# Passes over the ones in the dense part that take their limits from a step on what their block has formed

## The chip, the cores and the metric

The kernel runs on one NeuronCore of a Trainium2 chip. Its engines are PE (TensorE, matrix products and transposes), DVE (VectorE), ACT (ScalarE), POOL (GpSimd) and SP, which issues transfers. The metric is the device time of one launch in microseconds, less is better. Before the change the median of three runs is 2996.88 us (2996.64 to 3000.27).

## What is computed

Four graph layers over 4096 nodes with 256 features share one adjacency matrix of 4096 x 4096 integers. Layer 0 is an attention layer with a dense tail (two normalised hidden layers, a softmax over 128 states and a gate); layer 1 is a mean over neighbours, so it needs the number of ones of each row; layers 2 and 3 are attention layers.

```python
# layer 0, after attention gave h_attn
h_enh = silu(_ln(Wh @ fe1_w + fe1_b, ...)) @ fe2_w + fe2_b
B, C, dt = split(Wh @ W_bcdt + b_bcdt, 3)
ab = softmax(dt + A) * B @ abp_w + abp_b
h_part, z = split((Wh * ab) @ W_hz + b_hz, 2)
hs = ((h_part * silu(z) + h_part * D) @ out_w + out_b) * (1 + C @ cp_w + cp_b)
g = sigmoid(silu(_ln(concat(h_attn, hs) @ g1_w + g1_b, ...)) @ g2_w + g2_b)
out = _ln(g * h_attn + (1 - g) * hs + h_enh, ...)
# layer 1
a = (adj == 1); deg = sum(a, axis=1)
out = (a @ x / deg) @ W.T + b
```

## The kernel before

The rows lie in 32 tiles of 128; four tiles are a block, so there are NB = 8 blocks. Layer 0 first does its attention (to about 624 us), then the dense part, block by block (`dense`, from line 720), then layer 1 follows from about 1220 us.

**The dense part.** `dense(b)` is a generator of some 30 steps. In order it turns the projected rows (`whT`, lines 683 and 687), forms `bc` (line 744) and the exponent of the softmax (line 753), forms `t1` for the hidden layer (line 770) and its normalisation (`fe_off`, `fe_rs`), turns `bc` into `abT` (line 781 then forms `hsT`), turns the normalised `t1` into `zT` with SiLU on ACT (line 710), forms `sz` in two halves (ACT in line 794, POOL in line 797, DVE in line 803), `henh` (line 812) and `hs` (line 819), `comb` (line 684 on ACT, line 687 on DVE), `t2` (line 840) and its normalisation (`gl_off`), again `zT` for the gate, the gate's product and `tanh` (lines 852 to 858), the last normalisation (`ol_off`, line 699 on ACT) and two additions on POOL (lines 861 and 862). `run_staggered(..., 16)` starts a new block every 16 steps, so that the second half of block b-1 stands beside the first half of block b. In the text a pair is such a pair of halves.

**The passes over the ones.** The number of ones of a row is found beside all this. A quarter is 128 rows by 1024 columns of the adjacency matrix. POOL issues its transfer (line 173), and ACT makes two passes over it (line 180): each takes the sign of (value + limit) with the limits -0.5 and -1.5, and adds it up into `over`. Half the difference of the two sums is the count. The first COUNTED = 22 tiles, 88 quarters or 176 passes, are done in the dense part, the others in layer 1. Four buffers hold quarters (AHEAD = 4), one buffer the signs. `with_counts` calls one quarter at each of the first 11 steps of a block (lines 883 to 888).

**What sets the order.** The program is written as above, but the compiler's scheduler fixes the order in each engine's queue, by the dependencies and its own estimate of when each input is there. A pass depends on nothing but its transfer, the buffers and the constant `limits`, so it may be placed ahead of other steps of its block. Each engine then works its queue in that order and waits where an input is late. PSUM buffers matter for PE: three for transposes (`tp`), five for products (`mm`).

Of the kernel before, what the change touches and what calls it, by code (L numbers as in the profile page):

```python
# [11 lines left out]
F32 = mybir.dt.float32  # L12
# [4 lines left out]
ALU = mybir.AluOpType  # L17
# [4 lines left out]
P = 128  # L22
# [6 lines left out]
def run_staggered(gens, period):  # L29

    gens, active, tick = list(gens), [], 0
    while gens or active:
        if gens and tick % period == 0:
            active.append(gens.pop(0))
        for g in list(active):
            if next(g, StopIteration) is StopIteration:
                active.remove(g)
        tick += 1
# [3 lines left out]
def kernel(ctx: ExitStack, tc: tile.TileContext, w: dict, out: bass.AP):  # L42
    nc = tc.nc
# [3 lines left out]
    KD = D // P  # L47
    BT = 4
    NB = NT // BT
# [38 lines left out]
    limits = const.tile([P, 2], F32, name="limits")  # L88
# [63 lines left out]
    def products(ps, lhsT_of, rhs_of, n):  # L152
        for k in range(n):
            nc.tensor.matmul(  # L154
                out=ps, lhsT=lhsT_of(k), rhs=rhs_of(k), start=(k == 0), stop=(k == n - 1)
            )
# [4 lines left out]
    class Tally:  # L161
# [10 lines left out]
                )  # L172
                nc.gpsimd.dma_start(out=self.came[-1], in_=adj[ts(t, P), ts(q, QW)])  # L173

        def count(self, g):
            self.ask(g + self.bufs - 1)
            t, q = self.asked[g]
            for v in range(2):
                sign = self.pool.tile([P, QW], BF16, tag="sign", name="sign", bufs=1)
                nc.scalar.activation(  # L180
                    sign, self.came[g], AF.Sign, bias=limits[:, v : v + 1],
                    accum_out=over[:, t, v, q : q + 1],
                )
# [240 lines left out]
    with ExitStack() as l0:  # L424
# [10 lines left out]
        with ExitStack() as es:  # L435
# [157 lines left out]
            with ExitStack() as ps_:  # L593
                wp = ps_.enter_context(tc.tile_pool(name="l0_w0", bufs=1))
                work = ps_.enter_context(tc.tile_pool(name="l0_prep", bufs=2))
                small = ps_.enter_context(tc.tile_pool(name="l0_ps", bufs=4))
# [51 lines left out]
        with ExitStack() as es:  # L648
            d = es.enter_context(tc.tile_pool(name="l0_d", bufs=1))
            code_p = es.enter_context(tc.tile_pool(name="l0_code", bufs=AHEAD))  # L650
            small = es.enter_context(tc.tile_pool(name="l0_s", bufs=4))
# [27 lines left out]
            def turn(dst, parts, take):  # L679

                ps = pst.tile([P, BW], F32, tag="tp", name="tp")
                for i, part in enumerate(parts):
                    nc.tensor.transpose(ps[:, ts(i, P)], part, ident)
                take(dst, ps)
# [19 lines left out]
            def hidden(z, g, b):  # L704

                zT = d.tile([P, KI, BW], F32, tag="zT", name="zT", bufs=2)
                for k in range(KI):
                    turn(
                        zT[:, k, :], [z[:, i, ts(k, P)] for i in range(BT)],
                        lambda dst, ps: nc.scalar.activation(  # L710
                            dst, ps, AF.Silu, scale=g[:, k : k + 1], bias=b[:, k : k + 1]
                        ),
                    )
                    if k % 2:
                        yield
                return zT

            tally = Tally(code_p, AHEAD, 0, COUNTED)

            def dense(b):  # L720
                at = ts(b, BT)
# [6 lines left out]
                whT = d.tile([P, KD, BW], F32, tag="whT", name="whT", bufs=2)  # L728
                for k in range(KD):
                    turn(  # L730
                        whT[:, k, :], [wh[:, b * BT + i, ts(k, P)] for i in range(BT)],
                        onto,
                    )
                yield
                if b == NB - 1:
                    v0.close()
# [29 lines left out]
                t1 = d.tile([P, BT, DI], F32, tag="t", name="t", bufs=2)  # L766
                for i in range(BT):
                    ps = psm.tile([P, DI], F32, tag="mm", name="mm")
                    products(ps, lambda k: whT[:, k, ts(i, P)], lambda k: fe1[:, k, :], KD)
                    nc.vector.tensor_tensor(t1[:, i, :], ps, fe1_b, ALU.add)  # L770
                    if i % 2:
                        yield
                yield from normed(t1, "fe")
                abT = parts[1, BW][:, 0, :]
                turn(abT, [dt[:, i, :] for i in range(BT)], onto)
                yield
                hsT = parts[KD, BW]
                for k in range(KD):
                    ps = psm.tile([P, BW], F32, tag="mm", name="mm")
                    products(ps, lambda _: abp[:, 0, ts(k, P)], lambda _: abT, 1)  # L780
                    nc.vector.scalar_tensor_tensor(
                        hsT[:, k, :], ps, abp_b[:, k : k + 1], whT[:, k, :], ALU.add, ALU.mult
                    )
                yield
                a1T = yield from hidden(t1, fe_g, fe_b)

                sz = d.tile([P, KI, BW], F32, tag="sz", name="sz")
# [12 lines left out]
                for k in range(KI):  # L800
                    ps = psm.tile([P, BW], F32, tag="mm", name="mm")
                    products(ps, lambda e: whz[:, e, ts(k, P)], lambda e: hsT[:, e, :], KD)
                    nc.vector.scalar_tensor_tensor(
                        sz[:, k, :], ps, hz_b[:, k : k + 1], sz[:, k, :], ALU.add, ALU.mult
                    )
                    if k % 2:
                        yield
                henh = d.tile([P, BT, D], F32, tag="henh", name="henh")
                for i in range(BT):
                    ps = psm.tile([P, D], F32, tag="mm", name="mm")  # L810
                    products(ps, lambda k: a1T[:, k, ts(i, P)], lambda k: fe2[:, k, :], KI)
                    nc.vector.tensor_tensor(henh[:, i, :], ps, fe2_b, ALU.add)
                    if i % 2:
                        yield
                hs = d.tile([P, BT, D], F32, tag="hs", name="hs")
# [65 lines left out]
                    pass  # L881

            def with_counts(b):
                n = COUNTED * NQ // NB
                for k, _ in enumerate(dense(b)):
                    if k < n:
                        tally.count(b * n + k)
                    yield

            tally.ask(AHEAD - 2)  # L890
            run_staggered([with_counts(b) for b in range(NB)], 16)

# [52 lines left out]
    with ExitStack() as es:  # L947
# [10 lines left out]
        small = es.enter_context(tc.tile_pool(name="l1_s", bufs=4))  # L958
# [21 lines left out]
        tally = Tally(over_a, AHEAD, COUNTED, NT)  # L980
# [131 lines left out]
    with ExitStack() as l3:  # L1112
# [4 lines left out]
        with ExitStack() as es:  # L1117
            wp = es.enter_context(tc.tile_pool(name="l3_w", bufs=1))
            work = es.enter_context(tc.tile_pool(name="l3_prep", bufs=2))
            small = es.enter_context(tc.tile_pool(name="l3_ps", bufs=4))  # L1120
# [54 lines left out]
        small = l3.enter_context(tc.tile_pool(name="l3_small", bufs=4))  # L1175
# [165 lines left out]
```

## Time and profile before

| | |
|---|---|
| median of 3 runs | 2996.88 us |
| the profiled execution | 2998.89 us, of which the span 2997.0 us |
| PE busy over the span | 2864.1 us (96%) |
| DVE, ACT, POOL busy | 1878.5, 1282.4, 954.4 us (63, 43, 32%) |
| passes (line 180), all 256 | 293.8 us on ACT, 218 us of them in the dense part |
| dense part, first to last block | about 625 to 1220 us |

The page's second part cuts the span into 40 slices of 75 us, and gives each engine's busy share in tenths. The dense part fills slices 9 to 16:

```profile
PE   6989999999999999899999999999999999999999
DVE  5877666425555554477688788646766566566653
ACT  5765656459997223793163444333212112111211
```

ACT is nearly full in slices 10 to 12 and mostly idle in 14 to 16, while PE is busy in all of them. A busy PE is not a PE at its peak: the ends of matmuls are modelled, and a wait inside a group of matmuls can be counted as busy. So stages are compared by how long the same matmuls take in them. Where the passes fall is seen in windows of one pair each, for the passes of line 180 alone (columns: window and length, ACT busy and instructions, the clock granted to PE, the share of the DMA engines, GB/s; each pass is two instructions):

```profile
630.00:704.00 74.00, 56.68 (x91) 0.98 0.62 92
704.00:778.00 74.00, 50.57 (x83) 1.00 0.52 79
778.00:852.00 74.00, 50.05 (x81) 0.98 0.52 79
852.00:926.00 74.00, 48.77 (x81) 0.98 0.52 79
926.00:1000.00 74.00, 12.18 (x20) 0.98 0.08 18
1000.00:1070.00 70.00, 0.00 (x0) 1.00 0.02 8
1070.00:1140.00 70.00, 0.00 (x0) 1.00 0.03 8
```

### The profile page before, as it was taken

What the parts mean: (1) busy time and instruction counts of PE and PEld (TensorE: products, weight loads), DVE (VectorE), ACT (ScalarE), POOL (GpSimd) and SP (SyncE); (2) the same over time, 40 slices, a digit from 0 to 9 for tenths busy, and PEclk for the clock granted to TensorE, in tenths of its full rate; (3) what the DMA queues carried; (4) which work ended last, traced back from release to release, by engine and by line L of the source; (5) the groups of instructions that cost most, each with busy time, mean ns of one, the idle gap of its engine ahead of it and who ended that gap; (6) DMA issues with size and microseconds to landing.
All of it is one profiled execution on the core that took longest, in us unless ns stands there. A gap on an engine that the chain in (4) does not pass through costs nothing.

```text
span 2997.0 us, 35132 instructions
## 1 busy us (share of the span) xinstructions
PE 2864.1 (96%) x13357; PEld 2334.0 (78%) x13357; DVE 1878.5 (63%) x3456; ACT 1282.4 (43%) x1961; POOL 954.4 (32%) x718
## 2 busy tenths in 40 slices
PE   6989999999999999899999999999999999999999
PEld 5778888866555666687877788888888888888888
DVE  5877666425555554477688788646766566566653
ACT  5765656459997223793163444333212112111211
POOL 4666665534554333220044655550000000000000
PEclk9999999999999999999999999999999999999999
DMA  6966665245553000496332222101111111111100
GB/s 145 213 147 128 132 133 136 67 64 77 78 78 53 8 8 8 122 241 174 123 148 85 78 78 78 43 12 61 64 44 54 38 34 62 39 34 62 34 8 8
DMA packets 109473, 239.41 MB, mean 80 GB/s; under 512 B 10780, under 2 KB 31256, under 8 KB 100600
## 3 DMA queue, kind: packets, MB, share of 16 engines
q1 hardware_dynamic: 68936, 165.44, 15.9%
q0 software_dynamic: 37696, 69.11, 15.4%
q10 hardware_dynamic: 2672, 2.62, 0.3%
q8 instruction: 105, 1.72, 0.2%
q14 instruction: 64, 0.52, 0.1%
HBM read 266.42 MB, written 37.81 MB: 102 GB/s over the span
## 4 chain that ended last, share of the span: by engine, by line
PE 63%; ACT 9%; issue 8%; POOL 7%; DVE 7%; DMA 5%; POOLq 0%; ACTq 0%; DVEq 0%; SPq 0%
PE acc L368 16%; PE acc L1273 15%; PE s L154 15%; PE mm L154 9%; PE acc L1006 5%; POOL y L330 4%; ACT sign L180 4%; DVE run L275 3%; DVE y L326 2%; DMA a<-in_adj_dram 1%; DMA ab_row<-l_ab_d 1%; ACT y L357 1%; DMA turned<-codesT 1%; ACT turned L493 1%; PE q_ps L154 1%
## 5 line engine op out<-in xcount | busy, mean ns | idle before, releaser
L368 PE MATMUL acc<-v,y 128*128 128x257 f32 x4096 | 932.8, 386 | 24.5 <-ACT hp L917 16.0
L368 PEld LDWEIGHTS acc<-v,y 128*128 128x128 f32 x4096 | 774.6, 192 | 139.6 <-ACT hp L917 21.3
L330 POOL TENSOR_TENSOR y<-y,turned 128x1024 f32<-128x1024 f32 (+1 forms) x272 | 550.0, 2036 | 315.5 <-DVE y L326 269.4
L357 ACT ACTIVATE y<-y,sdst 128x512 f32<-128x512 f32 (+1 forms) x544 | 350.8, 689 | 357.3 <-POOL y L330 357.2
L326 DVE SCALAR_TENSOR_TENSOR y<-ab_row,cdst,b 128x512 f32<-128x512 f32 (+1 forms) x544 | 366.4, 710 | 168.8 <-PE acc L368 105.4
L1273 PE MATMUL acc<-v,y 128*128 128x257 f32 x2048 | 454.5, 380 | 0.4 <-DVE rden L1281 0.4
L154 PE MATMUL s<-qT,hT 128*128 128x256 f32 x2048 | 445.2, 379 | 0.7 <-ACT qT L1221 0.7
L1266 ACT ACTIVATE y<-y 128x1024 f32<-128x1024 f32 x128 | 132.2, 1055 | 714.3 <-DVE y L1265 710.1
L154 PEld LDWEIGHTS s<-qT,hT 128*128 128x128 f32 x2048 | 389.2, 190 | 54.0 <-ACT qT L1221 1.4
L1273 PEld LDWEIGHTS acc<-v,y 128*128 128x128 f32 x2048 | 387.3, 190 | 55.7 <-issue 0.8
L180 ACT ACTIVATE sign<-a,limits 128x1024 bf16<-128x1024 bf16 x256 | 293.8, 1148 | 27.2 <-DMA a<-in_adj_dram 21.6
L1235 DVE SCALAR_TENSOR_TENSOR y<-code,s 128x512 f32<-128x512 bf16 x256 | 175.8, 687 | 100.9 <-PE s L154 100.7
L275 DVE SCALAR_TENSOR_TENSOR run<-turned,dst,run 128x512 f32<-128x512 bf16 x248 | 186.7, 753 | 42.1 <-DMA turned<-codesT 37.4
L275 DVE SCALAR_TENSOR_TENSOR run<-turned,v,run 128x512 f32<-128x512 bf16 (+1 forms) x279 | 192.9, 691 | 24.2 <-ACT turned L493 18.5
L1265 DVE TENSOR_TENSOR y<-y,top 128x1024 f32<-128x1024 f32 x128 | 146.2, 1214 | 43.0 <-PE top L1259 43.0
L1242 DVE TENSOR_TENSOR mx<-mx,y 128x512 f32<-128x512 f32 x224 | 154.9, 691 | 7.4
L493 ACT ACTIVATE turned<-cT,log_wide 128x1024 bf16<-128x1024 bf16 x128 | 140.9, 1101 | 30.9 <-PE cT L488 30.6
L1006 PE MATMUL acc<-early,eq 128*128 128x512 f32 x512 | 129.1, 401 | 10.7 <-issue 9.1
L154 PE MATMUL mm<-kept 128*128 128x512 f32 x288 | 136.7, 612 | 1.6 <-DVE kept L687 0.8
L173 POOL DMA_DIRECT2D a<-in_adj_dram x128 | 76.1, 596 | 190.8 <-ACT sign L180 158.2
L1006 PEld LDWEIGHTS acc<-early,eq 128*128 128x128 f32 x512 | 96.8, 190 | 34.3 <-issue 11.2
L1006 PE MATMUL acc<-late,eq 128*128 128x512 f32 x512 | 122.5, 391 | 0.0
(233 smaller groups left out, 2988.9 us busy)
## 6 DMA issues: line engine op xcount, KB each, us to landing
turned<-codesT SPq DMA_DIRECT2D x36, 1024.0 KB
adj_t<-in_adj_dram POOLq DMA_DIRECT2D x128, 256.0 KB, 4.6
codesT<-turned SPq DMA_DIRECT2D x32, 1024.0 KB
a<-in_adj_dram POOLq DMA_DIRECT2D x128, 256.0 KB, 4.7
code<-codesT SPq DMA_DIRECT2D x128, 256.0 KB
code<-codesT SPq DMA_DIRECT2D x64, 512.0 KB
ab_row<-l_ab_d SPq DMA_DIRECT2D x15, 512.0 KB
xt<-in_x_dram SPq DMA_DIRECT2D x8, 512.0 KB
```

The source lines that it names most:

```text
L154: nc.tensor.matmul(out=ps, lhsT=lhsT_of(k), rhs=rhs_of(k), start=(k == 0), stop=(k == n - 1))
L180: nc.scalar.activation(sign, self.came[g], AF.Sign, bias=limits[:, v : v + 1], accum_out=over[:, t, v, q : q + 1],)
L275: nc.vector.scalar_tensor_tensor(st["run"], code, dst, st["run"], ALU.subtract, ALU.min)
L326: nc.vector.scalar_tensor_tensor(y[:, :, k, :], st["ab"][:, 0, :, :], self.cdst[:, c + k : c + k + 1], st["b"], ALU.add, ALU.max,)
L330: nc.gpsimd.tensor_tensor(y, y, mask[:, :, c % QT : c % QT + 2, :], ALU.subtract)
L357: nc.scalar.activation(y[:, :, k, :], y[:, :, k, :], AF.Exp, bias=self.sdst[:, c + k : c + k + 1],)
L368: nc.tensor.matmul(out=acc, lhsT=y[:, r, k, :], rhs=self.v[:, c + k, 0 : D + 1], start=(c + k == 0), stop=(c + k == NT - 1),)
L493: nc.scalar.activation(ct.rearrange("p c i -> p (c i)"), ps, AF.Exp, scale=math.log(UNIT / WIDE), bias=log_wide,)
L1006: nc.tensor.matmul(out=acc, lhsT=eqs[c // (NT // 2)][:, ts(c % (NT // 2), P)], rhs=v1[c // BT][:, c % BT, :, :], start=(c == 0), stop=(c = ...
L1235: nc.vector.scalar_tensor_tensor(y[:, :, c : c + 2, :], st["code"][:, :, c : c + 2, :], -BIG / UNIT, ps, ALU.mult, ALU.add,)
L1242: nc.vector.tensor_tensor(mx, mx, y[:, :, c : c + 2, :], ALU.max)
L1273: nc.tensor.matmul(out=accs[r], lhsT=st["y"][:, r, c, :], rhs=v3[:, c, :], start=(c == 0), stop=(c == NT - 1),)
```

## The change

A quarter's two passes no longer take the constant `limits` as bias. For each quarter DVE writes a tile `held` of 128 x 2 from the two limits and from two columns of the value its block formed last (`reached[b]`): the step is min(value >= 0, limit), which gives the limit itself, as the first operand is 0 or 1 and both limits are negative. So the result is the same, and a pass must wait until its block has come so far. `reached` is set behind `whT`, the `t1` rows, `abT`, `hsT`, the second half of `sz` and the `henh` rows. `held` has four buffers. The 11 quarters of a block are also dealt out differently: quarter g of a block goes to step k with 11k/16 <= g < 11(k+1)/16, so that they take the first 16 steps instead of the first 11.

```diff
-        def count(self, g):
+        def count(self, g, limits=limits):
             self.ask(g + self.bufs - 1)
...
+            APART = 16
+            reached = {}
...
+                reached[b] = whT[:, KD - 1, 0:2]
                 yield
...
                     nc.vector.tensor_tensor(t1[:, i, :], ps, fe1_b, ALU.add)
+                    reached[b] = t1[:, i, 0:2]
...
                 turn(abT, [dt[:, i, :] for i in range(BT)], onto)
+                reached[b] = abT[:, 0:2]
...
+                reached[b] = hsT[:, KD - 1, 0:2]
                 yield
                 a1T = yield from hidden(t1, fe_g, fe_b)
...
+                    reached[b] = sz[:, k, 0:2]
...
+                    reached[b] = henh[:, i, 0:2]
...
                 n = COUNTED * NQ // NB
                 for k, _ in enumerate(dense(b)):
-                    if k < n:
-                        tally.count(b * n + k)
+                    for g in range(k * n // APART, min((k + 1) * n // APART, n)):
+                        held = small.tile([P, 2], F32, tag="held", name="held")
+                        nc.vector.scalar_tensor_tensor(
+                            held, reached[b], 0.0, limits, ALU.is_ge, ALU.min
+                        )
+                        tally.count(b * n + g, held)
                     yield
 
             tally.ask(AHEAD - 2)
-            run_staggered([with_counts(b) for b in range(NB)], 16)
+            run_staggered([with_counts(b) for b in range(NB)], APART)
```

## The prediction

> **What bounds the kernel now.** I read the page's slices first: the passes over the ones (the `L180` rows) run on ACT in the dense part, from 630 us to about 950 us, and the rest in layer 1. Then the windows of the dense part, to compare block pairs that carry passes with pairs that carry none. The page's row gives the price of a pass:
>
> ```profile
> L180 ACT ACTIVATE sign<-a,limits 128x1024 bf16<-128x1024 bf16 x256 | 293.8, 1148 | 27.2 <-DMA a<-in_adj_dram 21.6
> ```
>
> A block pair is the time from one gate normalisation to the next: block b runs its first steps beside the last steps of block b-1. Away from one stretch the pairs are alike. From the first `comb` matmul to the transposes of `bc` PE takes 20.6 us with or without passes (753.40 to 774.00, 1046.16 to 1066.76). The stretch that differs begins at the transposes of `bc` and ends where PE takes up the `hz` matmuls again after the first half of the gate matmuls (`zT`). Its windows in six of the seven pairs, in order (start:end and length, busy time and instructions of PE, its weight loads, DVE, ACT and POOL, then the clock, the DMA share and GB/s):
>
> ```profile
> 702.51:717.50 14.99, 13.84 (x66) 8.79 (x65) 4.24 (x9) 14.89 (x23) 4.11 (x4) 1.00 0.15 22
> 774.00:791.56 17.56, 15.26 (x66) 9.58 (x64) 4.24 (x9) 16.47 (x25) 4.11 (x4) 0.90 0.20 29
> 848.05:866.03 17.98, 15.40 (x65) 9.76 (x64) 4.24 (x9) 16.07 (x24) 4.11 (x4) 0.91 0.17 25
> 922.53:938.81 16.28, 13.90 (x66) 8.76 (x64) 4.24 (x9) 16.19 (x25) 4.11 (x4) 1.00 0.20 30
> 997.04:1010.44 13.40, 13.33 (x65) 8.89 (x64) 4.24 (x9) 10.37 (x15) 3.79 (x3) 1.00 0.00 0
> 1066.76:1080.16 13.40, 13.33 (x65) 8.90 (x64) 4.24 (x9) 10.44 (x15) 3.79 (x3) 1.00 0.00 1
> ```
>
> The same 65 or 66 matmuls take 13.4 us where ACT has no passes and 15.0 to 18.0 us where it is full. The excess of the four is 1.6 + 4.2 + 4.6 + 2.9 = 13.2 us. The timelines of PE and ACT in the second window show why:
>
> ```profile
> 772.06 2.92 ACT L699 ACTIVATE t<-t,fe_off,fe_rs 128x512 f32<-128x512 f32 x4
> 774.88 1.13 ACT L180 ACTIVATE sign<-a,limits 128x1024 bf16<-128x1024 bf16 x1
> ...
> 778.67 1.28 ACT L710 ACT_TABLE_LOAD   x1
> 779.96 0.78 ACT L710 ACTIVATE zT<-tp,c_fe_ln_b,c_fe_ln_g 128x512 f32<-128x512 f32 x1
> 780.64 2.92 ACT L699 ACTIVATE t<-t,gl_off,gl_rs 128x512 f32<-128x512 f32 x4
> ...
> 781.50 0.44 PE L683 MATMUL tp<-ident,t 128*128 128x128 f32 x2 [2.00 <-ACT t L699]
> ```
>
> Three passes (774.88 to 778.67, 3.8 us) stand between the normalised `t` and the table load, and PE stands idle 2.00 us for the gate's `t`. In a pair without passes the same ACT work is one run with gaps of 1.6 us in all, and PE does not wait for it:
>
> ```profile
> 1063.32 2.93 ACT L699 ACTIVATE t<-t,fe_off,fe_rs 128x512 f32<-128x512 f32 x4 [14.35 <-DVE fe_off L696]
> 1066.27 1.28 ACT L710 ACT_TABLE_LOAD   x1
> ...
> 1070.59 2.93 ACT L699 ACTIVATE t<-t,gl_off,gl_rs 128x512 f32<-128x512 f32 x4 [1.31 <-DVE gl_off L696]
> ```
>
> So PE bounds the dense part, and passes cost only where they stand ahead of ACT's work between `fe_off` and the last `zT`. Passes elsewhere are free: in 817 to 891.5 us ACT is busy 69.5 of 74.5 us, and outside the stretch that pair loses 0.2 us. One more loss of 1.9 us follows the last passes: 938.81 to 976.44 takes 37.6 us against 35.7 us from 1010.44 to 1046.16. It comes with a PE gap of 2.07 us before 969.9, after which the clock is at 0.78 to 0.80 until 976. In all, 15.1 us is lost to passes before.
>
> [...] This trace shows lower clocks after shorter gaps (2.00, 2.50 and 2.07 us) and none after 1.84 us[...].
>
> **The change part by part.** The number of passes, their size and their DMAs stay: 11 quarters a block, 22 passes. What changes is their place. The bias of a pass comes from a DVE step that reads what the block has just formed, so a pass cannot be put ahead of its block. Before, 176 passes were through by 950 us, about 40 to each pair; now each of seven pairs gets 22, up to the last.
>
> *The order on ACT.* The instruction order of the changed kernel, which the program fixes, has in a steady pair, from `fe_off`: one fe `t`, pass, three fe `t`, table load, zT fe, pass, one gl `t`, pass, three gl `t`, zT fe, pass, zT gl, pass, zT gl, two zT fe, pass, zT gl, pass, zT gl, three `sz`, pass, `sz`, pass. Seven passes stand before the last zT where before there were three. The reason is in the code: quarters five to seven of a block all hang on `hsT`, formed just there.
>
> *ACT's walk.* Clock zero is the end of `fe_off` (1063.23 in the pair without passes; there the last zT ends at 14.9 and PE reaches the transposes of `bc` at 3.5). Start 0.4 (0.1 as there, and 0.3 for a new step on DVE ahead of `fe_off` and its handover); eight `t` at 0.705 (2.82 for four, 772.06 to 774.88) 5.64; table load 1.28; eight zT at 0.67 5.36; seven passes at 1.15 (770.91 to 772.06) 8.05. Sum 20.7. Each zT's transposes are there in time, as PE is ahead of ACT.
>
> *PE's walk.* PE's order was changed as well: it takes two of the `hz` matmuls and eight transposes of `wh` earlier, into the waits. After the last zT it still has two gate matmuls of 0.43, two of 0.86 and eight of 0.43, 6.0 us, and 0.15 for the handover, so it ends them at 26.9. In the pair without passes this point is at 1087.05, or 23.8, and 0.87 us of `wh` transposes come later; so the loss is 2.2 us.
>
> *The end of the pair.* One pass stands between the third and the fourth `xs` normalisation (`ol`), 1.15 us on the way to POOL's `L861` and `L862`. With the 3.1 us by which the gate matmuls end later and 0.2 us for a DVE step, `L862` ends at 46.5 instead of 42.05. From there to the first `comb` matmul the trace has 10.6 us (1105.27 to 1115.88); 1.3 us of `whT` copies and 0.4 us of the first `hs` step no longer lie in it. So it starts at 55.4 instead of 52.65, a lag of 2.8 us. Ten passes after that normalisation end at 50.3, before `comb`'s copy is wanted at 51.7. Seven pairs: 19.6 us.
>
> *The DVE steps.* 88 steps of 128x2; the nearest row (`fe_off`, 128x4) takes 0.16 us, so 14 us on an engine busy half of the time in the dense part. They cost something only ahead of `fe_off` and `ol_off`, and there they are in the walk. Lower bound nothing, upper 0.3 us at each. A step also waits for the pass that last read its buffer, four quarters before, and holds DVE's queue. The tightest is the next block's first step: its pass ends at 42.8, and the `pl_st` behind it waits for POOL until 46.5 anyway. POOL's DMA issues (0.6 us each) wait for passes four quarters before; the one ahead of `gl_rs` needs a pass that ends at 2.3, and `gl_rs` is due at 6.
>
> *The first block.* `exp` stands behind two passes instead of four (635.86 to about 632.8), but POOL's `obc` until 637.1 takes over as the bound of `bc` (638.03), 0.9 us at most; a pass among the fe `t` gives most back. I take -0.5 us, between -0.9 and +0.3.
>
> **The sum.** 19.6 - 15.1 - 0.5 = +4.0 us on a span of 2997.0 us: 3001.0. The profiled execution took 2998.89 us in all, 2.0 us above the median of the runs, 2996.88 us; on the median the forecast is 3000.9 us.
>
> **Rivals.**
> *The clock falls in every pair (slower).* PE has a gap of about 1.9 us ahead of the second `hs` transpose, and gaps of 2.0 us and more were followed by a lower clock, which cost 1.6 us at 968. From 2.0 us on, seven pairs pay 7 x 1.6 = 11 us: 3012 us. For it: the gap is at the edge; against it: 1.83 us at 1041 and 1111 passed unharmed.
> *The run of ten passes is late (slower).* If the `ol` step is 1.5 us or more later than in the walk, `comb`'s copy waits behind passes and each pair loses 1 us more: 3008 us.
> *PE hides more (faster).* If the work moved into the waits covers them to a loss of 1.0 us a pair, then 7.0 - 15.1 - 0.5 = -8.6 us: 2988 us. For it: the first pair before lost just 1.6 us with three passes. Against it: the seven passes are in ACT's one chain.
> *The passes don't spread.* The new wait might leave them bunched. The order on ACT is fixed and has 22 to a pair, so this is unlikely; the time would stay at 2997 us.
>
> **How the numbers follow.** Forecast 0.45 (loss of 1.9 to 3.4 us a pair, -2 to +8 us, 2995 to 3005 us); clock 0.18; late run 0.12; faster 0.20; no spreading 0.05. Within 0.2% (6 us, about what a measurement of this kernel can tell from no change): 0.37 of the forecast's own, 0.02 of the faster case and 0.05, 0.44. Slower: 0.08 + 0.18 + 0.12 = 0.38. Faster: 0.18. The range 2989 to 3014 us leaves out part of the faster case and the clock case with the late run on top.
>
> **What would show it.** From the `bc` transposes to the end of the gate matmuls all seven pairs should take about 23.4 us (20.3 us without passes before, 1066.76 to 1087.05), with 7 to 9 passes in each. ACT should be about 70% busy to the end of the dense part, against 95% and then 30%. A pair should take 72 to 73 us. I am wrong if pairs take under 71 us or over 74, or if PE waits longest for DVE steps on `held`.

## The result and the profile after

The changed kernel takes 3025.15 us (3023.98 to 3027.17), against 2996.76 us before (2994.95 to 3000.27) in the same comparison: a ratio of 1.0095 (95% interval 1.0082 to 1.0107). The forecast was 3000.9 us, with a range of 2989 to 3014. The profiled execution has a span of 3024.9 us, 27.9 us more than before.

The passes spread as the order of the queues said. The page of the changed kernel has ACT evenly busy through slices 9 to 16, where it was nearly full and then idle; the second line is a row of its groups (count, then busy us and mean ns, then the idle time ahead of them and what ended most of it):

```profile
ACT  5766555356666666594254344433212111111211
...
L180 ACT ACTIVATE sign<-a,held 128x1024 bf16<-128x1024 bf16 x176 | 201.5, 1145 | 116.7 <-DVE held L898 75.6
```

The new row says that ACT waited 75.6 us for `held`. That is idle time of an engine with time to spare, and by itself says nothing of a cost. The windows of the passes alone, one from each transposing of `bc` to the next (columns as before: window and length, ACT busy and instructions, clock, DMA share, GB/s), have 22 passes in each and very different lengths:

```profile
705.37:778.49 73.12, 27.24 (x44) 1.00 0.28 47
778.49:855.78 77.29, 27.19 (x44) 0.93 0.27 45
855.78:928.93 73.15, 27.23 (x44) 1.00 0.29 47
928.93:1003.50 74.57, 27.20 (x44) 0.98 0.28 46
1003.50:1081.30 77.80, 27.23 (x44) 0.96 0.27 44
1081.30:1156.11 74.81, 27.23 (x44) 0.98 0.28 46
```

Same work, and a spread of 4.7 us that goes for the most part with the clock (the fifth also has a long wait on POOL, below). The first and the third, at full clock, are undisturbed pairs of this kernel: 73.1 us, against 69.7 us for a pair without passes before. The stretch from the transposes of `bc` to the end of the gate matmuls is the forecast's own measure. Its windows in the same pairs (busy time and instructions of PE, weight loads, DVE, ACT, POOL, then the clock):

```profile
705.37:728.82 23.45, 21.92 (x98) 14.54 (x97) 6.53 (x17) 21.70 (x34) 8.37 (x8) 1.00 0.30 46
778.49:803.36 24.87, 23.33 (x98) 15.37 (x97) 6.53 (x17) 21.80 (x34) 9.32 (x9) 0.93 0.29 43
855.78:879.24 23.46, 21.92 (x98) 14.53 (x97) 6.53 (x17) 21.68 (x34) 8.36 (x8) 1.00 0.30 45
928.93:953.81 24.88, 23.34 (x98) 15.36 (x97) 6.53 (x17) 21.80 (x34) 9.32 (x9) 0.93 0.28 43
...
1081.30:1104.75 23.45, 21.92 (x98) 14.54 (x97) 6.53 (x17) 21.68 (x34) 8.36 (x8) 1.00 0.30 45
```

It was forecast at 23.4 us and takes 23.45 us in four of these six pairs, the one left out here among them; the other two ran at a clock of 0.93. So the loss that was worked out is there, and something is added to it. Two places show what. The first is POOL's queue at the last normalisation. In the timeline of the changed kernel (start, length, line, what, count, and in brackets the idle time before it and what ended it) POOL waits 5.36 us with a transfer of a quarter, for the passes that free its buffer, and `ol_rs` stands behind that:

```profile
813.51 0.60 POOL L173 DMA_DIRECT2D a<-in_adj_dram  x1 [5.36 <-ACT sign L180]
814.13 1.06 POOL L117 TENSOR_TENSOR ol_rs<-ol_ve,mhalf 128x4 f32<-128x4 f32 x1
```

Its input `ol_ve` was there at 813.21. In the pair without passes before, POOL waited for that input and began at once:

```profile
1097.07 1.04 POOL L117 TENSOR_TENSOR ol_rs<-ol_ve,mhalf 128x4 f32<-128x4 f32 x1 [5.07 <-DVE ol_ve L114]
```

From the end of `tanh` to the end of `ol_off` takes 10.5 to 10.7 us in six pairs where it took 9.53 without passes, and 12.6 us in one. The second is the end of the pair on PE, in the timeline of the changed kernel:

```profile
823.88 1.04 PE L683 MATMUL tp<-ident,xs 128*128 128x128 f32 x8
825.58 0.33 PE L683 MATMUL tp<-ident,hs 128*128 128x128 f32 x1 [0.66 <-DVE hs L827]
827.58 1.26 PE L683 MATMUL tp<-ident,hs 128*128 128x128 f32 x3 [1.68 <-DVE hs L827]
...
830.35 4.99 PE L154 MATMUL mm<-bcw,whT 128*128 128x257 f32 x14
```

and two windows around it (columns as in the stretch):

```profile
823.70:827.10 3.40, 1.54 (x11) 1.04 (x9) 2.21 (x12) 3.33 (x5) 1.57 (x3) 1.00 0.57 168
827.10:833.90 6.80, 6.32 (x18) 4.87 (x19) 3.35 (x8) 2.63 (x5) 5.85 (x5) 0.50 0.68 107
```

PE waits twice for `hs`, is busy for 1.54 of 3.40 us, and the next 6.8 us run at half clock: the 14 matmuls take 5.0 us, where they took 3.2 in a pair without passes before:

```profile
1043.12 3.21 PE L154 MATMUL mm<-bcw,whT 128*128 128x257 f32 x14
```

Through the dense part the clock stands at 0.50 for nine units of 3.4 us, where before it did for four.

The 27.9 us, read from the two traces by the same events: 21.9 in the seven pairs (from the first transposes of `bc` to the first `comb` matmul of the last pair, 500.2 against 478.2 us), 1.4 in the first block, 1.7 in a half-clock window while the last `comb` matmuls run, 1.65 in a longer gap ahead of layer 1 (10.79 against 9.14 us), and 1.45 because the dense part starts later, at 626.09 instead of 624.64 us; what follows takes 0.3 us less. The last two are not put down to the change: in the fourteen kernels profiled here that start lies between 622.7 and 629.3 us and that gap between 8.6 and 10.8 us. What follows the dense part takes 1757.0 to 1761.1 us in all of them.

### The profile page after: what moved, and what is told of

It is laid out like the page before. It is cut to its first block, busy times and chain, and to the rows that moved or that the text cites. A ratio compares the mean times of both kernels' runs of the same rounds, so it can differ in the third digit from the quotient of the medians.

```text
span 3024.9 us, 35221 instructions
## 1 busy us (share of the span) xinstructions
PE 2879.2 (95%) x13357; PEld 2339.4 (77%) x13357; DVE 1895.6 (63%) x3544; ACT 1278.5 (42%) x1961; POOL 956.4 (32%) x718
## 3 DMA queue, kind: packets, MB, share of 16 engines
q0 software_dynamic: 37696, 69.11, 14.6%
## 4 chain that ended last, share of the span: by engine, by line
PE 67%; POOL 8%; ACT 7%; issue 7%; DVE 7%; DMA 3%; POOLq 0%; ACTq 0%; DVEq 0%; SPq 0%
PE acc L368 18%; PE acc L1287 15%; PE s L154 15%; PE mm L154 12%; POOL y L330 5%; PE acc L1020 4%; DVE run L275 2%; ACT sign L180 2%; DVE y L326 1%; ACT y L357 1%; PE tp L683 1%; PE q_ps L154 1%; ACT turned L493 1%; ACT t L699 1%; DMA ab_row<-l_ab_d 1%
## 5 line engine op out<-in xcount | busy, mean ns | idle before, releaser
L180 ACT ACTIVATE sign<-a,held 128x1024 bf16<-128x1024 bf16 x176 | 201.5, 1145 | 116.7 <-DVE held L898 75.6
L1020 PE MATMUL acc<-early,eq 128*128 128x512 f32 x512 | 128.8, 401 | 13.0 <-issue 10.8
```

The source lines that it names most:

```text
L180: nc.scalar.activation(sign, self.came[g], AF.Sign, bias=limits[:, v : v + 1], accum_out=over[:, t, v, q : q + 1],)
L1020: nc.tensor.matmul(out=acc, lhsT=eqs[c // (NT // 2)][:, ts(c % (NT // 2), P)], rhs=v1[c // BT][:, c % BT, :, :], start=(c == 0), stop=(c = ...
```

## The experiments

Theory A: the time is made by where the passes, and POOL's issues for them, stand in the queues. Its parts: passes ahead of the last `zT` (the stretch), D, an issue that holds `ol_rs` back, and E, gaps on PE that bring half-clock windows with them. Rival B: the dealing of 22 passes to every pair costs as such. Rival C: the DVE steps and the handover to ACT cost. F came up on the way. The table has the median, the 95% interval of the ratio to the kernel before, which ran again in each comparison (medians 2994.6 to 2998.7 us), the length of the dense part in the profiled execution (first `whT` transposes to the first matmul of layer 1) and the units of half clock (3.4 us each) between 640 and 1215 us.

| kernel | us | ratio, 95% | dense us | half-clock units |
|---|---|---|---|---|
| before | 2996.8 | | 612.4 | 4 |
| after | 3025.2 | 1.0082 to 1.0107 | 639.2 | 9 |
| e1 dealing only | 3007.8 | 1.0019 to 1.0045 | 622.7 | 6 |
| e2 constant bias by DVE | 3012.5 | 1.0031 to 1.0065 | 625.9 | 7 |
| e3 ask later | 3023.5 | 1.0074 to 1.0104 | 638.2 | 9 |
| e4 late release | 3029.0 | 1.0092 to 1.0122 | 644.1 | 16 |
| e5 early release | 3003.2 | 1.0017 to 1.0037 | 618.7 | 7 |
| e6 no issue ahead | 3008.9 | 1.0027 to 1.0061 | 626.3 | 12 |
| e7 stretch back | 3018.4 | 1.0057 to 1.0093 | 632.2 | 13 |
| e8 filled gap | 3019.0 | 1.0056 to 1.0109 | 629.8 | 3 |
| e9 neither | 2998.0 | 0.9988 to 1.0006 | 607.2 | 3 |
| e10 neither, filled | 3026.3 | 1.0076 to 1.0106 | 638.0 | 9 |
| e11 the same from PSUM | 2989.3 | 0.9968 to 0.9984 | 602.3 | 1 |
| e12 stretch only | 3018.9 | 1.0059 to 1.0089 | 635.9 | 14 |

**e1, the dealing alone.**

```diff
-                        held = small.tile([P, 2], F32, tag="held", name="held")
-                        nc.vector.scalar_tensor_tensor(
-                            held, reached[b], 0.0, limits, ALU.is_ge, ALU.min
-                        )
-                        tally.count(b * n + g, held)
+                        tally.count(b * n + g)
```

> Only the dealing of the change: 11 quarters over the first 16 steps of a block, but the passes take the constant limits and wait only for their DMA. On ACT the order of the steady pair is then the one of the kernel before (three passes in the stretch, about 40 to a pair, none later). Theory A, where the passes stand on ACT and POOL makes the 28 us: 2995 to 3000 us, as before. Rival B, it is the dealing, each block having its passes spread over more steps: 3015 to 3025 us.

3007.8 us, 9 us above before, which neither theory expected. The order of ACT's steps is the old one, but POOL's is not: before, one issue stood between `ol_rs` and the two additions; in e1 both stand behind them. The timeline of e1 on ACT shows what that does in a pair with many passes:

```profile
831.04 1.15 ACT L180 ACTIVATE sign<-a,limits 128x1024 bf16<-128x1024 bf16 x1 [1.62 <-DMA a<-in_adj_dram]
832.32 1.15 ACT L180 ACTIVATE sign<-a,limits 128x1024 bf16<-128x1024 bf16 x1
833.47 0.57 ACT L684 COPY comb<-tp 128x512 f32<-128x512 f32 x1
```

The eighth of nine passes waits for its quarter, the ninth and `comb`'s copy are late, and from the end of POOL's additions to the first `comb` matmul takes 12.2 to 12.8 us in three pairs, here 12.2, instead of 10.5. So a place on POOL, not only on ACT, is worth microseconds.

**e2, a constant bias by way of DVE.**

```diff
-                            held, reached[b], 0.0, limits, ALU.is_ge, ALU.min
+                            held, limits, 0.0, limits, ALU.is_ge, ALU.min
```

> The changed kernel with all its 88 DVE steps and its buffers for held, but each step reads the constant limits instead of what the block has formed, so that a pass depends on a DVE step that can run at any time. The order of passes on ACT is that of e1. Theory A (places): 2996 to 3002 us. Rival C, the DVE steps and the handover from DVE to ACT cost the time (0.3 us for each of 88 quarters): 3020 to 3025 us.

3012.5 us. Of the 28 us the 88 DVE steps and their handovers, with the order of e1 on ACT, account for 4.7 us over e1, and the two intervals overlap. C in this form isn't what makes the 28 us. The price isn't nothing, though: sixteen of e2's steps in the dense part last 0.56 to 3.18 us beside POOL's work, which theory F below would explain, and 36 wait for a pass to free their buffer, 58.4 us in all.

**e3, asking later.**

```diff
-            self.ask(g + self.bufs - 1)
+            self.ask(g + self.bufs - 2)
```

> The changed kernel, asking for one quarter less ahead, so that the DMA issue ahead of ol_rs on POOL waits for a pass that ended one quarter earlier; the order of every queue stays. Theory A with its part D (the DMA issue holds ol_rs back, 0.74 us in each of seven pairs and 2.2 us more in one): 5 to 8 us under the changed kernel, 3017 to 3020 us, and ol_off ends 9.7 us after tanh instead of 10.5. Rival: ol_rs is not held by the issue, or the time comes back in a lower clock: within 2 us of 3025 us.

3023.5 us, no difference that the intervals tell. The edit didn't reach what it was meant for: the issue stands at the same place in POOL's queue and waits for the same pass (it begins at 812.68, 0.3 us after a pass ended), and tanh to `ol_off` stays at 10.47 us. It says nothing on D.

**e4, another dealing.** The changed kernel with its quarters at steps 1, 1, 1, 2, 2, 2, 11, 14, 15, 15, 15.

```diff
+            DEAL = (1, 1, 1, 2, 2, 2, 11, 14, 15, 15, 15)
...
-                    for g in range(k * n // APART, min((k + 1) * n // APART, n)):
+                    for g in [g for g, at in enumerate(DEAL) if at == k]:
```

> The changed kernel with another dealing: quarters at steps 1, 1, 1, 2, 2, 2, 11, 14, 15, 15, 15, so that 22 passes to a pair remain, all released by DVE steps, but none stands between fe_off and the last zT and none between the ol normalisations; they stand after tanh (2), after ol (6), beside comb (5) and after exp (9). Theory A: each pair comes back to 69.7 to 70.5 us, the sum to before less its loss of 15 us: 2979 to 2988 us. Rival C (the wait on a block's value costs wherever the pass stands): 3010 us or more. Rival B (22 passes in every pair cost as such): 3010 us or more.

3029.0 us: the expectation fell. The stretch did become free (the last `zT` ends at 15.0 us after `fe_off`, as without passes, and POOL's second addition at 43.0 instead of 47.1), but `comb` starts at 56.8 to 59.9 us in six pairs (56.0 to 60.7 in the changed kernel). The timelines of e4 on DVE, ACT and PE:

```profile
893.79 0.75 DVE L122 BATCH_NORM_STATS2 pl_st<-xs 128x6 f32<-128x256 f32 x2 [6.34 <-POOL xs L871]
...
895.33 0.39 DVE L820 TENSOR_TENSOR henh<-mm,kept 128x256 f32<-128x256 f32 x1
...
895.75 0.23 DVE L899 SCALAR_TENSOR_TENSOR held<-henh,limits 128x2 f32<-128x2 f32 x2
```

```profile
896.00 1.15 ACT L180 ACTIVATE sign<-a,held 128x1024 bf16<-128x1024 bf16 x1 [7.10 <-issue]
...
903.51 0.56 ACT L684 COPY comb<-tp 128x512 f32<-128x512 f32 x1
```

```profile
904.13 0.66 PE L683 MATMUL tp<-ident,hs 128*128 128x128 f32 x4 [3.27 <-ACT comb L684]
```

The last `henh` step, on which six passes hang, stands on DVE behind `pl_st`, which waits 6.34 us for POOL. So ACT idles for 7.1 us until those steps are through, then has six passes (7.5 us) ahead of the copy that PE needs. A release is only as early as the queue of the engine that gives it.

**e5, the same released early.** As e4, but with no `reached` on `henh`, and with twelve buffers for `held`.

```diff
-                    reached[b] = henh[:, i, 0:2]
...
-                        held = small.tile([P, 2], F32, tag="held", name="held")
+                        held = small.tile([P, 2], F32, tag="held", name="held", bufs=12)
```

> The dealing of e4 (steps 1, 1, 1, 2, 2, 2, 11, 14, 15, 15, 15), but no pass hangs on a henh step any more (those quarters hang on the last sz step) and held has 12 buffers, so that no release stands behind DVE's wait for POOL and DVE waits for no pass. On ACT: none before the last zT, three after tanh, seven after ol, one between the comb copies, four and seven around exp. Theory A, corrected by e4 (what counts is whether ACT has passes left when comb's copy is wanted): the six passes of e4 that ran from 896 to 903.5 start at about 889, comb's copy isn't late, comb starts 53.5 to 54.5 us after fe_off (58.5 in e4, 52.65 without passes); the sum is 2984 to 2996 us. Rival C (the wait on a block's value costs wherever the pass stands): 3015 us or more.

3003.2 us, 26 us less than e4 and 22 less than the changed kernel, though above the range given. Six pairs take 73.0 us in the mean (75.1 in the changed kernel), with `comb` at 52.0 to 55.0 us after `fe_off`. The two edits weren't tried apart: in e4 `held` steps also waited for passes, 12 times and 16.4 us in all, and in e5 none does. So how much of the 26 us is the place of the release and how much the buffers is open.

**e6, no issue ahead of `ol_rs`.** As e5, with steps 1, 1, 1, 2, 2, 2, 2, 14, 15, 15, 15.

```diff
-            DEAL = (1, 1, 1, 2, 2, 2, 11, 14, 15, 15, 15)
+            DEAL = (1, 1, 1, 2, 2, 2, 2, 14, 15, 15, 15)
```

> As e5, with the quarters at steps 1, 1, 1, 2, 2, 2, 2, 14, 15, 15, 15: now no DMA issue of a quarter stands ahead of ol_rs on POOL, one pass stands after tanh instead of three, and one stands among the four fe normalisations. Theory A with its part D (the issue holds ol_rs back): tanh to the end of ol_off takes 9.5 to 9.6 us as in pairs without passes, against 10.4 in e5; the pass among the fe steps gives 1.15 us to the last zT. Together 2984 to 2998 us. Without D: tanh to ol_off as long as in e5.

POOL's timeline in e5, then in e6:

```profile
808.43 0.64 POOL L173 DMA_DIRECT2D a<-in_adj_dram  x1 [5.37 <-ACT sign L180]
809.09 1.06 POOL L117 TENSOR_TENSOR ol_rs<-ol_ve,mhalf 128x4 f32<-128x4 f32 x1
```

```profile
808.43 1.03 POOL L117 TENSOR_TENSOR ol_rs<-ol_ve,mhalf 128x4 f32<-128x4 f32 x1 [5.08 <-DVE ol_ve L114]
```

In e5 `ol_ve` was there at 808.14, 0.95 us before `ol_rs` could start; in e6 `ol_rs` starts 0.08 us after it. From tanh to `ol_off` takes 9.53 us in e6 and 10.5 us in e5: D is shown, at 0.98 us a pair. The time is no better, 3008.9 us: with the pass among the `fe` steps the last `zT` ends at 14.6 to 17.2 us after `fe_off`, and five pairs have two units of half clock each.

**e7, the stretch put back.** As e5, with steps 1, 1, 1, 2, 7, 8, 10, 11, 14, 15, 15.

```diff
-            DEAL = (1, 1, 1, 2, 2, 2, 11, 14, 15, 15, 15)
+            DEAL = (1, 1, 1, 2, 7, 8, 10, 11, 14, 15, 15)
```

> As e5, but three quarters hang on hsT again (steps 1, 1, 1, 2, 7, 8, 10, 11, 14, 15, 15): four passes stand ahead of the last gate zT, where e5 has none, two among the sz steps, fewer after exp. Theory A: the last zT ends 4 x 1.15 = 4.6 us later (19.6 after fe_off instead of 15.0), the gate matmuls end 2 to 2.5 us later than in e5, 14 to 18 us over seven pairs on top of e5. Rival: the stretch is hidden and the end of the pair alone counts: within 4 us of e5.

3018.4 us, 15.2 us more than e5, or 2.2 us a pair. The last `zT` ends at 18.8 us after `fe_off` (13.5 to 14.9 in e5), the gate matmuls at 25.15 (22.4 to 23.9), 1.3 to 2.7 us later. So passes in the stretch delay PE by about what was expected. The 15.2 us aren't the stretch's alone, though: e7 has 13 units of half clock where e5 has seven, and no run tells the two apart.

**e8, a gap filled.** In the changed kernel, with its own dealing, the `xs` transposes are made three times; the extra ones write the same values into the same PSUM bank.

```diff
-            def turn(dst, parts, take):
+            def turn(dst, parts, take, times=1):
...
-                for i, part in enumerate(parts):
-                    nc.tensor.transpose(ps[:, ts(i, P)], part, ident)
+                for _ in range(times):
+                    for i, part in enumerate(parts):
+                        nc.tensor.transpose(ps[:, ts(i, P)], part, ident)
...
                         onto if k % 2 else nc.scalar.copy,
+                        3 if k < KD else 1,
```

> The changed kernel, with the transposes of the four xs tiles ahead of the hs transposes made three times into the same PSUM bank (16 more transposes a block, 2.1 us of PE in the gaps of 0.7 and 1.7 us before the hs transposes; the values stay). Theory E, the windows of half clock near the end of a pair follow from PE being idle there: the windows at 827, 1052 and 1131 us vanish, xs to comb takes 9 to 9.5 us in every pair, 5 to 9 us less than the changed kernel: 3016 to 3020 us. Rival, the clock follows something else: the same windows and 3025 us, or more by the added work.

On PE, the timeline of e8 at the place shown above for the changed kernel:

```profile
821.72 2.78 PE L684 MATMUL tp<-ident,xs 128*128 128x128 f32 x24
824.34 0.27 PE L684 MATMUL tp<-ident,hs 128*128 128x128 f32 x1
825.44 1.55 PE L684 MATMUL tp<-ident,hs 128*128 128x128 f32 x7 [0.82 <-DVE hs L828]
826.82 3.64 PE L154 MATMUL mm<-bcw,whT 128*128 128x257 f32 x16
```

PE does 16 needless transposes a block, and the half-clock units fall from nine to three; one is left at the end of a pair (1049.4). The span of the profiled execution is 3015.1 us, 9.8 less than the changed kernel's for six units: 1.6 us each. The median is 3019.0 us, 6 us less, but its interval is too wide to set it apart. E is shown by this trace, one execution; its size in time only roughly.

**e9, neither pass nor issue in the way.** As e5, with steps 1, 1, 1, 1, 2, 2, 2, 14, 15, 15, 15.

```diff
-            DEAL = (1, 1, 1, 2, 2, 2, 11, 14, 15, 15, 15)
+            DEAL = (1, 1, 1, 1, 2, 2, 2, 14, 15, 15, 15)
```

> As e5 with the quarters at steps 1, 1, 1, 1, 2, 2, 2, 14, 15, 15, 15: no pass ahead of the last zT, none between the ol normalisations, no DMA issue of a quarter ahead of ol_rs, one pass after tanh, seven after ol, nine after exp. Theory A with D: tanh to ol_off 9.5 us (10.5 in e5), no pass in the stretch (17 us from fe_off to zT in e6 back to 13.5 to 15.0), so 4 to 7 us less than e5 if the windows of half clock are as many: 2993 to 3000 us, no better than before. Rival: the nine passes after exp or the held steps beside POOL's work cost as much as is saved: 3001 us or more.

2998.0 us, the time of the kernel before, with 22 passes in each pair, each released by a DVE step on what its block has formed. So B and C are refuted as causes of the 28 us: 22 passes to a pair, with steps and waits of this kind, cost no more than the passes did before once they stand elsewhere. They aren't free: the first six pairs have no half-clock window and take 70.3 to 71.6 us, against 69.7 us without passes.

**e10, the same with the gap filled.** As e9, with `turn` as in e8 and steps 1, 1, 1, 1, 1, 2, 2, 2, 14, 15, 15; of the two `xs` tiles it is here the first that is turned five times, which makes as many extra transposes as in e8.

```diff
-            DEAL = (1, 1, 1, 1, 2, 2, 2, 14, 15, 15, 15)
+            DEAL = (1, 1, 1, 1, 1, 2, 2, 2, 14, 15, 15)
...
                         onto if k % 2 else nc.scalar.copy,
+                        5 if k == 0 else 1,
```

> Quarters at steps 1, 1, 1, 1, 1, 2, 2, 2, 14, 15, 15, and the xs transposes made three times as in e8: the order on ACT as in e9, with PE busy while it waits for the hs steps. Theories A, D and E together: e9 less 1.4 us for each window of half clock that vanishes at the end of a pair (four to six): 2986 to 2995 us, which would beat the kernel before. Rival: the five held steps that stand ahead of comb's copies on DVE, beside POOL's xt, hold those copies back by 1.7 us a pair: 2998 us or more.

3026.3 us; the rival named there holds, and more of it than stated. The timelines of e10 on DVE, POOL and PE:

```profile
831.48 4.83 DVE L900 SCALAR_TENSOR_TENSOR held<-whT,limits 128x2 f32<-128x2 f32 x5
836.23 0.68 DVE L688 COPY comb<-tp 128x512 f32<-128x512 f32 x1
```

```profile
830.92 2.35 POOL L731 TENSOR_TENSOR xt<-xt,kept 128x1024 f32<-128x1024 f32 x1 [2.05 <-DMA xt<-in_x_dram]
...
833.85 2.35 POOL L843 TENSOR_TENSOR dh<-xs,hs 128x1024 f32<-128x1024 f32 x1
```

```profile
836.96 1.12 PE L684 MATMUL tp<-ident,hs 128*128 128x128 f32 x4 [4.37 <-DVE comb L688]
```

Five steps of 128x2 take 4.83 us, and two of them nearly all of it: one ends at 833.28, with POOL's `xt` step (833.27), the other at 836.23, with its `dh` step (836.20). `comb`'s copy stands behind them, and PE waits 4.37 us for it. That gave theory F: a DVE step with both operands in SBUF (`whT`, `limits` and `held` lie there; the tiles that PE writes, `tp` and `mm`, lie in PSUM) lasts until POOL's step ends. The 4.83 us alone don't show that it is the place of the operands; that was the author's guess, and e11 tests it.

**e11, one operand from PSUM.** `reached[b]` of step 1 is the PSUM tile from which `whT` was copied.

```diff
+                def noted(dst, src):
+                    onto(dst, src)
+                    reached[b] = src[:, 0:2]
...
                         whT[:, k, :], [wh[:, b * BT + i, ts(k, P)] for i in range(BT)],
-                        onto,
+                        noted,
                     )
-                reached[b] = whT[:, KD - 1, 0:2]
```

> As e10 with one change: the quarters of step 1 take their DVE step from the PSUM tile that whT was copied from, and no longer from whT in SBUF; the order of every queue is the one of e10. In e10 five such steps of 128x2 took 4.83 us beside POOL's xt and dh steps, and PE waited 4.37 us for comb. Theory F, a DVE step with both operands in SBUF lasts until POOL's step ends and one with an operand in PSUM does not: the five take 0.6 to 0.8 us, comb starts 2 to 4 us earlier in each pair (54.5 to 56.5 us after fe_off instead of 58 to 60), the sum is 3000 to 3012 us. Rival, the steps wait for something else (a buffer, a pass): still over 4 us, 3026 us.

2989.3 us, 37 us less than e10 for this edit alone, and faster than the kernel before (ratio 0.9976, 0.9968 to 0.9984). The same rows of the tile `held` from 700 to 1150 us (count, then shortest, median and longest ns), first e10's, then e11's:

```profile
L900 DVE SCALAR_TENSOR_TENSOR held<-whT,limits x30: 146/148/2886, 755.9 to 1139.7; 128x2 f32<-128x2 f32 x30
```

```profile
L904 DVE SCALAR_TENSOR_TENSOR held<-tp,limits x30: 146/149/151, 752.2 to 1102.1; 128x2 f32<-128x2 f32 x30
L904 DVE SCALAR_TENSOR_TENSOR held<-t,limits x18: 147/149/432, 766.3 to 1116.4; 128x2 f32<-128x2 f32 x18
```

The medians of the first two rows are the same, and the longest falls from 2886 to 151 ns, though all 30 steps of e11 begin while POOL's `xt` step runs. The third row, also of e11, has both operands in SBUF, and one of its long steps (766.30 to 766.73 us) ends with a POOL step again (766.71). F is shown, for an operand in PSUM beside POOL's `xt` step alone, for two in SBUF beside `xt`, `dh` and `bc`; beside POOL's `sz` step a step of the changed kernel with both in SBUF took 0.16 us (665.13 to 665.29 us). F is in other times too: `held` steps of up to 2.97 us in e5, e6 and e9 and 2.41 us in e12 stand in nearly every pair. In the changed kernel one of the 88 was that long, in the first block. All six whole pairs of e11 take 69.9 us, at full clock; a pair without passes took 69.7. One of them (columns as in the stretch):

```profile
847.64:917.58 69.94, 69.54 (x274) 45.02 (x272) 38.78 (x93) 48.13 (x75) 32.34 (x27) 1.00 0.29 50
```

**e12, the stretch alone.** In the changed kernel nothing but the steps of its quarters is altered.

```diff
+            DEAL = (1, 1, 1, 2, 2, 4, 5, 11, 13, 14, 15)
...
-                    for g in range(k * n // APART, min((k + 1) * n // APART, n)):
+                    for g in [g for g, at in enumerate(DEAL) if at == k]:
```

> The changed kernel with nothing but the steps of some quarters altered (1, 1, 1, 2, 2, 4, 5, 11, 13, 14, 15 instead of 1, 2, 4, 5, 7, 8, 10, 11, 13, 14, 15): no quarter hangs on hsT, three passes stand ahead of the last zT where the changed kernel has seven, none among the gate zT; the split of the ol normalisations and the DMA issue ahead of ol_rs stay. Theory A: the gate matmuls end 25 to 25.5 us after fe_off instead of 27 to 28.4, and 10 to 16 us of the 28 go: 3009 to 3015 us. Rival, the stretch is of no weight beside the end of the pair: 3020 us or more.

3018.9 us, 6 us less than the changed kernel; the two intervals overlap a little. The gain came where it was expected: the last `zT` ends at 16.1 us after `fe_off` instead of 20.6, the gate matmuls at 24.8 instead of 27.0 to 28.4, POOL's second addition at 44.9 instead of 47.1. Then it went: `comb` starts at 56.9 to 59.1 (56.0 to 60.7 in the changed kernel). The timelines of e12 on PE and DVE:

```profile
900.30 1.11 PE L683 MATMUL tp<-ident,xs 128*128 128x128 f32 x4 [3.62 <-DVE whT L687]
```

```profile
902.77 2.46 DVE L899 SCALAR_TENSOR_TENSOR held<-whT,limits 128x2 f32<-128x2 f32 x2
```

With the stretch free, PE's `wh` transposes went back behind the `sz` matmuls, so that it waits 3.62 us for DVE's copies; five pairs get two half-clock units each (14 in all, against nine), and two `held` steps take 2.46 us beside POOL. Seven pairs gained 15 us (7 x 2.2), and 6 are left: the end of the pair gave more than half back.

## Why the prediction was wrong

Two terms of its sum failed. The wait between `tanh` and `ol_off` was put at 0.2 us a pair and was 0.94 us, and 3.1 us in one; and the clock, which the sum put at nothing, cost 11.5 us. The parts in their order:

*What bounds the kernel, and the loss before.* Right. The loss to passes was put at 15.1 us; read by events, the seven pairs before lose 15.6 us against seven without passes.

*ACT's walk and PE's walk.* Right to 0.1 us where the clock is full: the last `zT` ends at 20.6 us after `fe_off` (forecast 20.7), the gate matmuls at 26.94 to 26.97 (26.9) in four pairs whose stretch ran at full clock. e7 moves the same point by four passes put back, though its time has half clock in it as well.

*The end of the pair.* Here the first term was mis-sized. The pass among the `ol` normalisations costs 1.14 us (1.15), and from POOL's second addition to `comb` an undisturbed pair takes 8.95 us (8.9). But "0.2 us for a DVE step" between tanh and `ol_off` is 0.94 us, and 3.1 in one pair. The prediction looked at the DMA issue that stands ahead of `gl_rs` and not at the one ahead of `ol_rs`; there DVE's release, ACT's pass, POOL's issue and `ol_rs` form a chain across three queues. Over seven pairs that is 7.5 us; e6 against e5 shows the usual part of it. Why the one issue waited 7.5 us for nothing that the trace names stays open.

*The clock.* The larger term, and a choice: it was a rival at 0.18, since the gaps foreseen were just under 2.0 us. The chance was set by the length of one gap. Seven units of half clock fall into the seven pairs, where before there were three; worked out from the events the seven cost 9.8 us, and 1.7 us more come with an eighth, while the last `comb` matmuls run. The rival's 11 us were right in size, but not as one window a pair: two of the first six pairs have none and two have two or three. The window ahead of 789.6 shows that the length of single gaps was the wrong measure: no gap in it is over 1.2 us, but PE is busy for 1.96 of 3.42 us, and half clock follows. e8 shows the tie.

*The DVE steps.* Their price of 0.16 us holds for 80 of 88; seven take 0.35 to 0.43 us and one 2.78 us, so apart from that one they are not what costs. It lies in the first block, beside POOL's steps, and the first block lost 1.4 us where a gain of 0.5 was forecast; how much of that is this step isn't shown.

*The sum.* 4.0 us forecast; to it come 7.5 for POOL's issue, 9.8 and 1.7 for the clock, 1.9 for the first block, 1.65 ahead of layer 1 and 1.45 for the later start of the dense part: 28.0 us. Some 1 us for the last pair and what was forecast a little too high elsewhere about cancel.

*The sign.* "Slower" had 0.38 and "the same" 0.44. All that came on top of the likeliest case was of one sign, a queue that gains a wait or the clock that follows one; the rival in which PE hides more did not come true. Of the signs of being wrong that were named, one did: four of the six whole pairs take over 74 us.

Not settled: what the stretch costs apart from the clock in the whole time (e7, e12), why e1 loses as much as 10 us in its dense part (the late quarter explains about 1.7 us in a pair with many passes, and it has two units of half clock more than before), whether the 4.7 us between e2 and e1 are anything, and at which busy share of PE the clock falls: in the dense part before, units in which PE was busy for up to 0.45 of the time were followed by half clock and none with 0.46 or more; in the changed kernel it followed such with 0.55 and 0.57, and didn't follow others with 0.49 and 0.51.

## What to carry to other kernels

In this kernel a dependence added to spread work over a chain had to be worked through queue by queue: the releasing step, the released one and the transfer that waits for the released one's buffer each held up what stood behind them in their engine's queue. Price each such place, not only the one on the busiest engine. Put the release on a value that is formed early on a queue with nothing waiting ahead of it, so that the released work fills time in which the bounding engine needs nothing from that engine (e9 against the changed kernel: 27 us). Where PE has short gaps, count its busy share over some 3.4 us; a few needless transposes in the gap took six of nine half-clock units away (e8), though the time gained, 6 us, lies within the noise of those runs.

## What the runs showed of the hardware

- A DVE step of 128x2 with two SBUF operands lasted up to 2.89 us beside POOL steps of 128x1024, which took 2.35 us, and 0.15 us with one operand in PSUM (e10, e11). The three long ones read singly ended 0.01 to 0.03 us after a POOL step.
- The clock had two values in the traces before and after the change, 1.00 and 0.50, in units of 3.41 us on a fixed grid: half clock began, among other places, at 782.48, 857.57 and 970.21 us before, 22 and 33 units apart, and at 789.60, 827.14 and 939.78 us after, 11 and 33 units apart. The values between the two in the prediction (0.78, 0.80, 0.90) are means over a window. In the changed kernel half clock also followed units in which PE was busy for 0.44 to 0.57 of the time.
- Where the units begin made a difference: two neighbouring pairs of the changed kernel with the same gaps ahead of `hs` (0.66 and 1.67 us, and 0.66 and 1.68 us) took 73.1 and 77.3 us, the first without half clock and the second with three units of it. In the unit that ends inside the longer gap PE was busy for 2.06 of 3.41 us in the first (748.64 to 752.05 us) and for 1.51 of 3.41 us in the second (823.73 to 827.14 us), and two of the three stand right behind the latter. The grids of the two traces lie 0.3 us apart.
